# Attention terms on another DMA queue, and first scores behind the reciprocals, in the early batches of a two-layer graph kernel

## The chip, the cores and the metric

The kernel runs on one core of a Trainium2 chip. The metric is the device time of one execution in microseconds, lower is better. TensorE (PE in the profile) multiplies matrices, VectorE (DVE), ScalarE (ACT) and GpSimd (POOL) do element-wise work, SyncE (SP) issues DMA transfers and computes nothing. Each engine works through its own queue of instructions in order. ScalarE and GpSimd can issue DMA transfers too, from the same queue in which their computation stands.

## The reference

x has shape (64, 256, 256): 64 batches of 256 nodes with 256 features; adj is one 256x256 adjacency matrix for all of them. Two layers follow each other, each of a graph attention and a feed-forward part on normalised rows:

```python
x = x + _L0_gnn_ref(_layernorm(x), adj, L0_gnn_W, L0_gnn_a)      # 4 heads of 64
x = x + _L0_ffn_ref(_layernorm(x), L0_ffn_weight, L0_ffn_bias)
x = x + _L1_gnn_ref(_layernorm(x), adj, L1_gnn_W, L1_gnn_a)      # 1 head of 256
x = x + _L1_ffn_ref(_layernorm(x), router_w, w1, b1, w2, b2)     # 2 of 8 experts a row
```

The part that the change touches is the attention of the first layer:

```python
e = e_src[:, :, None, :] + e_dst[:, None, :, :]
e = jnp.where(e >= 0, e, ALPHA * e)
e = jnp.where(mask, e, NEG_INF)
attn = jax.nn.softmax(e, axis=2)
h_prime = jnp.einsum('bijh,bjhd->bihd', attn, q)
```

The last part chooses the two experts of the eight with the highest router scores for each row and adds their outputs, weighted.

## The kernel before

**Tiles.** A batch is two tiles of 128 rows. Each batch is one generator, `batch_layers` (L554), that emits its instructions in about twenty parts. For the most part of the batches, rows are sent by indirect DMA to a region of memory for each expert (L1011), and pairs of 128 rows are fetched, multiplied and added to the output later (`expert_pair`, L829); the last few batches go through all experts densely.

**Order.** The order of instructions is written out by a small scheduler (L1194 to L1235). It works in steps, and a new batch begins every third step. Each active generator has a rank; in one step all of them advance by one part, in order of rank, the lowest first. `yield 10` means: my next part stands in the next step with rank 10. `yield -70` means: my next part stands still in this step, with rank 70. The order in which parts are emitted is the order in which every engine's queue holds them. Nothing of it is decided while the kernel runs.

**The parts of one batch that matter here**, by the step after the batch's begin:

- step 3: `projected` (L573, TensorE, exponentials on ScalarE), then with rank 24 `scaled` (L575, VectorE) and `send_terms` (L577), which turns a small tile ut on VectorE (L505). With rank 31 a DMA writes the 4 KB of ut to DRAM, to `terms` (L579). With rank 52 `spread_terms` (L586, the DMA at L514) reads them back to all 128 partitions, 512 KB into one half of the tile z. So each batch but the first has two DMAs on SyncE's queue for its terms, and the second reads what the first has written.
- step 5: with rank 10, `scores` of heads 0 and 1 (L589), with rank 70 those of heads 2 and 3 (L591). Each is four VectorE instructions at L530 that overwrite z. Batch 0 takes its terms from TensorE and has no such DMA.
- step 7: `attended` of the first layer with rank 50 (L594: TensorE, reciprocals rinv on VectorE at L551), then hp.
- step 8: e on ScalarE (L603), x1 on VectorE.
- steps 9 to 11: norm, transposes, the feed-forward product pf (L618), squares on ScalarE (L402), the copy of a transpose (L427, with rank 36).
- step 12: `projected1` of the second layer with rank 20 (L472; ex, q and me on ScalarE, L479 to L485).
- step 13: `scores1` with rank 25: transposes of ex on TensorE into pd (L491), z1 on VectorE (L496).
- step 14: `attended` of the second layer with rank 40 (L638), with its reciprocals at L551.
- step 15: rel on ScalarE with rank 5 (L644).
- step 18: xng (rank 29) and base (rank 50) on ScalarE (L671, L677).
- steps 19 and 20: the output's base is stored (L688), xng transposed and copied (rank 55), router scores (L702) and their copy lg (L706, rank 35).

Since batches begin three steps apart, step 5 of a batch falls into one step with step 2 of the next (rank 4: a transpose on VectorE), step 8 of the one before (rank 5), step 11 of the second before, step 14 of the third before (rank 40), and step 20 of the fifth before (rank 35). Likewise step 3 falls together with step 15 of the fourth before, step 12 of the third before and step 18 of the fifth before.

**Buffers.** z of the first layer has two buffers, ut one. All products on TensorE go to eight rotating banks of PSUM.

**Chunks and set-up.** `CHUNKS` gives how many batches are routed together: twelve chunks of 4, then smaller ones. Preparation of weights (`setup`, L328) is begun one piece a step from step 4; eight of the pieces are `pack_expert`, with four loads and one store on SyncE's queue each (L281 to L294).

Of the kernel before, what the change touches and what calls it, by code (L numbers as in the profile page):

```python
# [21 lines left out]
def rows_to_all(ap: bass.AP, n: int) -> bass.AP:  # L22

    return bass.AP(tensor=ap.tensor, offset=ap.offset, ap=[[0, P], [1, n]])
# [3 lines left out]
def kernel(  # L28
# [17 lines left out]
    nc = tc.nc  # L46
# [13 lines left out]
    CHUNKS = (4,) * 12 + (2,) * 5 + (1,) * 3  # L60
# [64 lines left out]
        return ap.rearrange("p (a k) -> p k a", k=KT)  # L125

    AHEAD, BLOCKS_AHEAD = 3, 2


    ident = const.tile([P, P], F32, tag="ident", name="ident")  # L130
# [357 lines left out]
    def scores1(ex, me):  # L488
        pd = bank("pd", [N])
        for t in range(NT):  # L490
            nc.tensor.transpose(  # L491
                pd[:, t * P : (t + 1) * P], ex[:, t, 1:2].to_broadcast([P, P]), ident
            )
        z = work.tile([P, NT, N], F32, tag="z1", name="z1", bufs=1)
        for j in range(NT):
            nc.vector.scalar_tensor_tensor(  # L496
                z[:, j, :], pd, ex[:, j, 2:3], me[:, j, :], op0=ALU.max, op1=ALU.mult
            )
        return [z[:, j, :] for j in range(NT)]

    def send_terms(q, b):


        ut = small.tile([P, S], F32, tag="ut", name="ut", bufs=1)
        nc.vector.transpose(  # L505
            ut.rearrange("p (t h w) -> p t h w", t=NT, h=H), q[:, :, :, HD - 1 : HD + 3]
        )
        ud = tc.dram_tile([S, S], F32, name=f"terms_{b}")
        ud = ud.rearrange("c r -> (c r)").rearrange("(c p) -> c p", p=P)
        return ut, ud  # L510

    def spread_terms(ud, z):

        nc.sync.dma_start(  # L514
            out=z[:, NT - 1].rearrange("p t h i -> p (t h i)"),
            in_=rows_to_all(ud, S * S),
        )

    def scores(q, z, hs, spread):

        for h in hs:
            terms = z[:, NT - 1, :, h, :]
            if not spread:
                terms = bank("pd", [NT, P])
                for t in range(NT):
                    nc.tensor.transpose(
                        terms[:, t, :], q[:, t, h, HD + 1 : HD + 2].to_broadcast([P, P]), ident
                    )
            for j in range(NT):
                nc.vector.scalar_tensor_tensor(  # L530
                    z[:, j, :, h, :], terms, q[:, j, h, HD + 2 : HD + 3],
                    masks[0][:, j, :].rearrange("p (t i) -> p t i", t=NT),
                    op0=ALU.max, op1=ALU.mult,
                )
# [19 lines left out]
    def batch_layers(b, c0, xng, lg):  # L554
# [21 lines left out]
        if b:  # L576
            ut, ud = send_terms(q, b)  # L577
            yield -31
            nc.sync.dma_start(  # L579
                out=ud.rearrange("c (g r) -> g c r", g=G),  # L580
                in_=ut[2 : P : S // (NT * H), :],
            )
            yield -52
        z = work.tile([P, NT, NT, H, P], F32, tag="z4", name="z4", bufs=2)
        if b:
            spread_terms(ud, z)  # L586
        yield 99
        yield 10
        scores(q, z, range(0, 2), b > 0)  # L589
        yield -70  # L590
        scores(q, z, range(2, 4), b > 0)  # L591
# [44 lines left out]
        z = scores1(ex, me)  # L636
# [527 lines left out]
    def jobs():  # L1164
        b = done = taken = 0
        for c, nb in enumerate(CHUNKS + (1,) * DENSE):
            nt = nb * NT
            lg = keep.tile([P, nt, E], F32, tag="lg", name=f"lg_{c}", bufs=7)
            xng = []
            row0 = b * N  # L1170
            done += nt
            n = max(done - (E - 1) - taken, 0) if b < ROUTED else 0
            taken += n
            for i in range(nb):
                def job(b=b, c=c, i=i, nb=nb, nt=nt, n=n, lg=lg, xng=xng, row0=row0):
                    yield from batch_layers(b, i * NT, xng, lg)
                    if i == nb - 1:
                        if b >= ROUTED:
                            yield 65
                            yield from route_dense(b, lg)  # L1180
                        else:
                            yield from route(c, row0, nt, n, b == ROUTED - 1, xng, lg)
                yield job()
                b += 1
# [86 lines left out]
```

## Time and profile before

| | |
|---|---|
| three runs | 1525.09, 1535.03, 1537.51 us, median 1535.03 |
| profiled execution | 1543.73 us, span 1542.0 us from the first to the last instruction |
| mean granted TensorE clock | 0.968 of full speed |
| TensorE busy | 1441.8 us, 94% of the span |
| VectorE busy | 1249.1 us, 81% |
| ScalarE busy | 1005.1 us, 65% |
| GpSimd busy | 878.5 us, 57% |
| DMA on the queue of SyncE | 322,828 packets, 171.6 MB |
| writes of terms (L579) and spreads (L514) | 63 each, all on SyncE's queue, median 545 and 350 ns to issue |

The page cuts the span into 40 equal slices; a digit is the busy share of a slice in tenths. Waits name the instruction that waited and the one whose end came last before it went on. In the order of time each row has the start, the length, the engine and line, the operation and its operands, and in brackets the idle time of the engine ahead of it. A small letter q behind an engine's name (SPq, ACTq) marks the engine's queue of DMA issues.

### The profile page before, as it was taken

To read this page: it belongs to the slowest core of one execution; us is meant where nothing else is said; L and a number is where in the kernel's file an instruction comes from. 1 tells how busy PE (TensorE), PEld (TensorE's weight loads), DVE (VectorE), ACT (ScalarE), POOL (GpSimd) and SP (SyncE) were. 2 spreads that over 40 slices of the span, in tenths; PEclk is the share of its full clock that TensorE was granted. 3 is DMA by queue.
4 is the path that set the end of the run, shared out by engine and by line. 5 is a ranking of instruction groups with operands and counts; after the bars stand their busy time and mean duration, and the time that the engine had idled before them with its cause. 6 is when DMAs were issued, how large, how long until landed. Compare 5 with 4: busy or idle time off the path is not lost. (4 is left out here: it accounts for less than half of the span.)

```text
span 1542.0 us, 29896 instructions
## 1 busy us (share of the span) xinstructions
PE 1441.8 (94%) x8066; PEld 1275.5 (83%) x8066; DVE 1249.1 (81%) x4392; ACT 1005.1 (65%) x2379; POOL 878.5 (57%) x853
## 2 busy tenths in 40 slices
PE   7889998999999999999999999998999988789994
PEld 5778787789999898999999989897878777578883
DVE  7779889889988988999889888899887887545542
ACT  1356556477777777777777777776677788544331
POOL 2212344445767766676757575856757677544444
PEclk9989899989999999999999999999999999889998
DMA  5744335557787887787878787867787676788743
GB/s 148 219 126 104 97 107 150 126 145 171 168 182 176 178 170 170 174 184 169 182 165 189 161 194 164 190 143 165 172 183 177 128 156 137 171 171 167 144 78 52
DMA packets 372852, 240.84 MB, mean 156 GB/s; under 512 B 264773, under 2 KB 334925, under 8 KB 372685
## 3 DMA queue, kind: packets, MB, share of 16 engines
q1 hardware_dynamic: 322828, 171.60, 45.2%
q0 software_dynamic: 48864, 66.33, 23.5%
q8 instruction: 67, 1.10, 0.3%
q10 hardware_dynamic: 992, 0.99, 0.2%
q14 instruction: 101, 0.82, 0.2%
HBM read 150.46 MB, written 88.35 MB: 155 GB/s over the span
## 5 line engine op out<-in xcount | busy, mean ns | idle before, releaser
L939 POOL DMA_INDIRECT out_dram<-y,xt x258 | 414.4, 1606 | 192.8 <-issue 63.8
L544 PE MATMUL pv<-q,z 128*128 128x65 f32 (+1 forms) x2560 | 375.0, 303 | 0.2
L544 PEld LDWEIGHTS pv<-q,z 128*128 128x128 f32 x2560 | 343.0, 200 | 12.5 <-DVE z L530 0.6
L1011 POOL DMA_INDIRECT xs<-xng,pos x244 | 266.7, 1093 | 65.3 <-issue 59.8
L918 PE MATMUL py<-w2s,hT 128*128 (+1 forms) x1224 | 285.4, 384 | 6.8 <-ACT hT L909 5.9
L918 PEld LDWEIGHTS py<-w2s,hT 128*128 128x128 f32 x1224 | 231.5, 193 | 39.8 <-ACT hT L909 8.4
L903 PE MATMUL ph<-sT,we 128*128 128x256 f32 x1032 | 240.5, 383 | 6.5 <-DVE sT L117 3.6
L530 DVE SCALAR_TENSOR_TENSOR z<-z,q,mask 128x256 f32<-128x256 f32 x504 | 232.3, 482 | 16.5 <-DMA z<-terms 7.5
L903 PEld LDWEIGHTS ph<-sT,we 128*128 128x128 f32 x1032 | 196.7, 192 | 34.6 <-DVE sT L117 4.4
L427 ACT COPY xT<-pt 128x512 f32<-128x512 f32 x192 | 113.5, 591 | 117.9 <-PE pt L421 93.1
L896 ACT ACTIVATE y<-y,w 128x256 f32<-128x256 f32 x258 | 113.1, 500 | 105.7 <-DVE y L928 98.0
L383 POOL TENSOR_SCALAR rstd<-mv 128x4 f32<-128x4 f32 (+1 forms) x67 | 15.9, 237 | 264.9 <-DVE mv L376 210.0
L909 ACT ACTIVATE hT<-ph,we 128x256 f32<-128x256 f32 x306 | 123.7, 473 | 61.4 <-PE ph L903 41.6
L472 PE MATMUL pq<-wx,xT 128*128 128x259 f32 x512 | 130.5, 398 | 19.0 <-ACT xT L427 15.0
L402 ACT ACTIVATE off<-x,sums 128x256 f32<-128x256 f32 x256 | 129.9, 507 | 16.9 <-DVE x L625 9.6
L928 DVE TENSOR_TENSOR y<-py,b2s 128x512 f32<-128x512 f32 x129 | 85.9, 686 | 58.8 <-PE py L918 45.0
L644 ACT ACTIVATE rel<-pv,rinv 128x256 f32<-128x256 f32 x128 | 53.6, 470 | 121.1 <-DVE rinv L551 95.5
L472 PEld LDWEIGHTS pq<-wx,xT 128*128 128x128 f32 x512 | 96.6, 195 | 41.9 <-ACT xT L427 22.0
L437 PE MATMUL pq<-wx,xT 128*128 128x268 f32 x512 | 128.6, 394 | 2.7 <-DVE xT L117 2.1
L618 PE MATMUL pf<-wfT,xT 128*128 128x256 f32 x512 | 129.4, 398 | 0.0
L437 PEld LDWEIGHTS pq<-wx,xT 128*128 128x128 f32 x512 | 98.6, 193 | 22.3 <-DVE xT L117 1.3
L618 PEld LDWEIGHTS pf<-wfT,xT 128*128 128x128 f32 x512 | 98.5, 203 | 12.3 <-issue 0.2
(164 smaller groups left out, 2373.5 us busy)
## 6 DMA issues: line engine op xcount, KB each, us to landing
we<-wpack SPq DMA_DIRECT2D x145, 288.0 KB
xr<-xs SPq DMA_DIRECT2D x516, 64.0 KB
z<-terms SPq DMA_DIRECT2D x63, 512.0 KB
xblk<-in_x_dram SPq DMA_DIRECT2D x256, 64.0 KB
xin<-in_x_dram SPq DMA_DIRECT2D x64, 256.0 KB
out_dram<-base SPq DMA_DIRECT2D x61, 256.0 KB
out_dram<-y,xt POOLq DMA_INDIRECT x258
xs<-xng,pos POOLq DMA_INDIRECT x244
```

The costliest lines, as they stand in the source:

```text
L402: nc.scalar.activation(off, src[:, t, :], AF.Square, bias=sums[:, t : t + 1], scale=-float(D), accum_out=sq[:, at + t : at + t + 1],)
L427: nc.scalar.copy(dst, pt)
L437: nc.tensor.matmul(pq.rearrange("p h c -> p (h c)"), xT[:, k, t * P : (t + 1) * P], wx[:, k, :], start=(k == 0), stop=(k == KT - 1),)
L472: nc.tensor.matmul(pq, xT[:, k, t * P : (t + 1) * P], wx1[:, k, :], start=(k == 0), stop=(k == KT - 1),)
L530: nc.vector.scalar_tensor_tensor(z[:, j, :, h, :], terms, q[:, j, h, HD + 2 : HD + 3], masks[0][:, j, :].rearrange("p (t i) -> p t i", t=N ...
L544: nc.tensor.matmul(pv[:, h, :], z(j, h, t), q[:, j, h, : d + 1], start=(j == 0), stop=(j == NT - 1),)
L618: nc.tensor.matmul(pf[:, t, :], xT[:, k, t * P : (t + 1) * P], wfT[:, k, :], start=(k == 0), stop=(k == KT - 1),)
L903: nc.tensor.matmul(ph[:, f, :], we[:, k * D + f * P : k * D + (f + 1) * P], xT[:, k, :], start=(k == 0), stop=(k == KT - 1),)
L909: nc.scalar.activation(hT[:, f, :], ph[:, f, :], AF.Gelu, bias=we[:, C_B1 + f : C_B1 + f + 1])
L918: nc.tensor.matmul(py[:, t, :], hT[:, f, t * P : (t + 1) * P], w2s[:, e, f * D : (f + 1) * D].rearrange("p e c -> p (e c)"), start=(f == 0 ...
L939: d = nc.gpsimd.indirect_dma_start(out=out_rows, out_offset=bass.IndirectOffsetOnAxis(ap=xt[:, t, 0:1].bitcast(I32), axis=0), in_=y[:, t, ...
L1011: d = nc.gpsimd.indirect_dma_start(out=xs_d[: E * CAP * PAIR, :], out_offset=bass.IndirectOffsetOnAxis(ap=at, axis=0), in_=xe, in_offset=None,
```

## The change

Two limits are computed from the chunks: `PAIRED` is 4 + 4 + 3 = 11, `SETTLED` is 16 + 2 = 18.

Both DMAs of a batch's terms, the write of ut and the spread into z, go to the queue of ScalarE (`nc.scalar`) in batches 1 to 17 and stay on that of SyncE from batch 18 on. Their ranks, 31 and 52, stay.

In batches 0 to 10 the scores of heads 0 and 1 get rank 42 in place of 10. In their step they then stand behind the second layer's reciprocals (rank 40) of the batch three before, and behind lg (rank 35) of the one five before. The scores of heads 2 and 3 keep rank 70.

```diff
     AHEAD, BLOCKS_AHEAD = 3, 2
+    PAIRED = CHUNKS[0] + CHUNKS[1] + 3
+    SETTLED = CHUNKS[0] + CHUNKS[1] + CHUNKS[2] + CHUNKS[3] + 2
...
-    def spread_terms(ud, z):
-
-        nc.sync.dma_start(
+    def terms_queue(b):
+
+        return nc.scalar if b < SETTLED else nc.sync
+
+    def spread_terms(b, ud, z):
+
+        terms_queue(b).dma_start(
             out=z[:, NT - 1].rearrange("p t h i -> p (t h i)"),
             in_=rows_to_all(ud, S * S),
         )
...
             yield -31
-            nc.sync.dma_start(
+            terms_queue(b).dma_start(
                 out=ud.rearrange("c (g r) -> g c r", g=G),
                 in_=ut[2 : P : S // (NT * H), :],
             )
             yield -52
         z = work.tile([P, NT, NT, H, P], F32, tag="z4", name="z4", bufs=2)
         if b:
-            spread_terms(ud, z)
+            spread_terms(b, ud, z)
         yield 99
-        yield 10
+        yield 10 if b >= PAIRED else 42
         scores(q, z, range(0, 2), b > 0)
         yield -70
         scores(q, z, range(2, 4), b > 0)
```

## The prediction

> **What bounds the kernel now.** I read the page's slices first, then clock and engines by stretch, and last the waits and the order of time of the first 450 us: the terms of batches 1 to 17 are issued from 22.8 to 280.1 us, so everything the change moves happens there.
>
> ```profile
> PE   7889998999999999999999999998999988789994
> ...
> PEclk9989899989999999999999999999999999889998
> ```
>
> A slice is 38.5 us. TensorE is full from slice 9 on, the first eight have gaps, and the granted clock dips there. The chain that ended last lies in the drain and says nothing of this start. Columns of the next view: the stretch, its length, busy us of PE, weight loads, VectorE, ScalarE, GpSimd, the granted clock, DMA share, GB/s.
>
> ```profile
> 77.70:81.10 3.40, 0.00 (x0) 0.00 (x0) 2.25 (x7) 0.29 (x1) 0.00 (x0) 1.00 0.78 272
> 81.10:91.30 10.20, 9.40 (x41) 8.92 (x42) 6.96 (x27) 5.98 (x17) 1.38 (x3) 0.50 0.75 209
> 91.30:169.90 78.60, 76.35 (x476) 67.20 (x476) 72.92 (x249) 50.25 (x141) 17.90 (x29) 1.00 0.37 90
> ```
>
> From 91 to 170 us VectorE works 72.9 of 78.6 us, and the order of time shows it without a gap over 0.31 us after 93 us: it is the bound there, TensorE follows. Reordering takes nothing from its work, so **only VectorE's own idle time can be won** before 200 us. It stands in two kinds of place: waits for terms, and waits for a TensorE at half clock. The order of time around the worst, SyncE's queue alone and then the engines:
>
> ```profile
> 69.90 0.53 SPq L579 DMA_DIRECT2D terms<-ut  x1
> 70.47 0.44 SPq L96 DMA_DIRECT2D xin<-in_x_dram  x1
> 74.06 0.34 SPq L514 DMA_DIRECT2D z<-terms  x1
> ```
>
> ```profile
> 78.77 1.92 DVE L530 SCALAR_TENSOR_TENSOR z<-z,q,mask 128x256 f32<-128x256 f32 x4 [5.70 <-DMA z<-terms]
> ...
> 80.81 0.84 ACT L644 ACTIVATE rel<-pv,rinv 128x256 f32<-128x256 f32 x2 [8.42 <-DVE rinv L551]
> ...
> 81.86 0.99 PE L491 MATMUL pd<-ident,ex 128*128 128x128 f32 x2 [5.16 <-ACT ex L479]
> ...
> 89.61 0.18 DVE L551 RECIPROCAL rinv<-pv 128x4 f32<-128x4 f32 x1 [2.81 <-PE pv L544]
> ...
> 92.78 0.48 DVE L625 SCALAR_TENSOR_TENSOR x<-pf,rstd,x1b 128x256 f32<-128x256 f32 x1 [1.67 <-PE pf L618]
> ```
>
> Batch 4's terms lie ready in ut at 66.1, but SyncE is busy with block loads and the packs of experts and sends them at 69.9; the spread waits for the write until 74.06. The bytes are back at 78.8. VectorE stands 5.70 us at the first scores; the second layer's reciprocals of batch 1 are behind them, so ScalarE's rel (8.42) and TensorE's transposes of ex (5.16) stand too. Then TensorE runs 10.2 us at clock 0.50, and VectorE waits for it twice more, 2.81 + 1.67 = 4.48 us. The sums of the first 450 us (total, times, longest):
>
> ```profile
> ACT rel L644 <- DVE rinv L551: 75.2, 21, 8.4
> ...
> ACT e L603 <- DVE hp L597: 25.2, 14, 7.6
> ...
> DVE z L530 <- DMA z<-terms: 7.5, 3, 5.7
> ```
>
> **What the Trainium skill says.** "DMA: Bandwidth & Descriptors", section Issuing engines are not separate DMA queues: transfers from any queue run on the same 16 engines and interleave; another issuing engine saves issue time alone. So I don't count on more bandwidth, only on leaving SyncE's line; no run here shows the interleaving yet. Same page, section Anatomy of one DMA: a semaphore wait is held by the issuing sequencer, not by the DMA engine. The trace agrees: in the same 450 us SyncE itself waits for terms at L514, 22.0 us in 24 times. "TensorE: Matmul & The Clock Gate", section Part 1: after an idle window of about 3.4 us the clock falls to half. The trace agrees: 77.7 to 81.1 is wholly idle, 81.1 to 91.3 has 0.50.
>
> **The change part by part.**
>
> 1. *Terms of batches 1 to 17 off SyncE's queue.* 34 DMAs move: 17 writes (median 545 ns of issue) and 17 spreads (350 ns). Waits for them: 1.63 us at 60.06 (batch 3), 5.70 (batch 4), 0.19 at 110.01 (batch 6), 7.5 in all. Batch 3: ut is ready at 50.4, SyncE wrote at 52.09, spread at 55.60. From ScalarE: written 50.4, spread by 53.9 at the latest (the 3.5 us SyncE needed), landed 4.5 later (55.60 to 60.06) at 58.4, which is when VectorE gets there. Gain 1.6. Batch 4: written 66.1, spread 1.7 (the usual step, 129.65 to 131.33) to 4.2 us later (69.90 to 74.06), landed 4.5 to 5.8 later (104.23 to 110.01): 72.3 to 76.1, against 73.1 when VectorE gets there. Gain 2.7 to 5.7; I take 4.5, as the DMA engines stay loaded with the packs. Sum **-6.1 us** (bounds 4 to 7.5).
>
> 2. *First scores behind the reciprocals, batches 1 to 10* (batch 0 too, which finds no second layer yet). Nothing is added: four instructions of L530, 1.91 us a group, change places with lg (0.17) and two reciprocals (0.22). The second pair of scores stays, so z is complete when it was. The new risk is a VectorE that waits for pv: ahead of the scores of batches 8 to 10, pv of the batch three before is done at 136.4, 150.9 and 166.4, and VectorE arrives at 136.85, 152.8, 168.8; no wait. rel and ex come up to 1.9 us earlier. TensorE's waits for ex then go (1.43 at 63, 5.16 at 82, 0.64 at 156, 1.67 at 172), but where VectorE is the bound this is worth nothing by itself. Its worth is the clock: without the idle 77 to 82, which part 1 alone would mostly remove as well, the half clock that follows goes and with it 4.48 us of VectorE's waits: **-4.5** (bounds 0 to 4.5). The stretch from 173.3 to 183.5, again at 0.50, follows a weaker gap, 1.47 + 0.20 of idle beside transposes, and costs VectorE 1.48 at 179.11 and 2.84 at 183.45, together 4.3. Windows fall by chance, so I take two thirds: **-2.9** (0 to 4.3; with the stretch at 193.7, another 0.44 + 2.42 = 2.9, it may be 7.2).
>
> 3. *What ScalarE pays.* 17 x (0.545 + 0.350) = 15.2 us of issue. ScalarE's five shapes of DMA at the start took 0.34 to 0.53, so bounds are 0.2 to 1.0 each. It also waits: for ut hardly, since its own xT copy ends as ut does (129.99 and 129.6 in batch 8); for the write to land 1.7 us, of which base (1.14, L677) covers most; take 0.5, in a loaded queue 2. That is 17 x 1.4 = 24 us on ScalarE. Queued behind it: the copy of xng's transpose (TensorE's router product waits), y of an expert, e (VectorE's L607), the squares (GpSimd's rstd), the copy before L472. The cover is idle time at just these: 25.2 us in 14 times before e, about 1.8 each, and the 3.6 a batch before rel. In batch 8's period e has only 0.26 of idle, the shift of 0.3 to 0.5 reaches the copy at 135.29, and TensorE is in pv until 136.44 while that copy ended at 135.85: hidden by 0.1 to 0.3 us. Batches 11 to 17 keep the old order and 1.7 us before e. Price on the path **+1** (bounds 0 to 10).
>
> 4. *What SyncE gains.* It no longer stands for ut with xin, base stores, xblk, packs and expert loads behind. No engine waits for those in this stretch beyond 1.0 us at the very start: **0**; POOL's queue is not passed.
>
> Sum: -6.1 - 4.5 - 2.9 + 1 = -12.5 us. From 320 us on TensorE is full and the program's order is fixed, so the shift should arrive at the end. The profiled execution took 1543.73 us (span 1542.0 and 1.7 around it), giving 1531.2; it is 8.7 above the median of 1535.03, and the median becomes **1522.5, say 1523**.
>
> **Rivals.** *The clock follows wholly*: the stretches at 81, 173 and 194 all vanish: -7.5 - 4.5 - 7.2 = -19, 1516. For it: each follows a wait for ex; against: batch 11, right before 194, keeps the old order. *The stall stays*: the packs saturate the DMA engines, the bytes land as late, and VectorE stands as before; only batch 3 and part of the clock are won: -3, 1532. *Slower: ScalarE held at the head of its queue.* Each of 17 batches has 0.9 of issue and 0.8 of wait (22.0/24 is 0.9 on SyncE) on ScalarE just ahead of e and the copies. If all is exposed, 17 x 1.7 = 29 less the 7.5 won is +21: 1556. It decides once the delay exceeds ScalarE's idle before e, 1.8 us on average but 0.26 in batch 8, and once TensorE's larger waits bring back half-clock stretches. Against: VectorE, not ScalarE, is the bound there. That the moves don't take effect at all I hold for very unlikely, as the order is written out.
>
> **Chances.** A measurement of this kernel can tell about 1%, 15 us, from no change. Forecast 0.52 (own range 1517 to 1530), clock follows 0.25, stall stays 0.12, slower 0.11. Faster by over 1% (under 1519.7): 0.25 and 0.12 of the forecast's, 0.37. Within 1%: 0.40 + 0.12 = 0.52. Slower: 0.11. The range from 1510 (the second case and 6 us, the spread of the runs shown) to 1538 (the third and 6) leaves out 2 in 10.
>
> **What would show it.** In the changed profile: L579 and L514 of early batches on ScalarE's queue, the write within 0.5 us of ut; no wait of z for terms over 2 us; rel's wait for rinv from about 3.6 down to under 2 us up to batch 10, and as before in 11 to 17; no idle of TensorE over 3 us near 80 and no clock of 0.5 right behind. Wrong if z still waits over 4 us, if the clock dips as often, or if ScalarE's copies make L472, e or hT late.

## The result, and the profile after

| | before | after |
|---|---|---|
| median, 20 runs each on one chip | 1533.6 us (1525.09 to 1546.77) | 1524.84 us (1517.67 to 1536.17) |
| ratio, with its 95% interval | | 0.9952 [0.9934, 0.9969] |
| profiled execution, and its span | 1543.73 us, 1542.0 us | 1526.76 us, 1525.0 us |
| mean granted TensorE clock in it | 0.968 | 0.976 |

The change makes the kernel 0.48% faster: less than the 1% bound of the prediction, yet an interval that leaves 1 out. Most lines stand six lower in the new file: z L536 (was L530), the write of ut L585 (L579), the spread L520 (L514), e L609 (L603), reciprocals L557 (L551), rel L650 (L644), while the copy xT is L429 (L427), the second layer's product L474 (L472), transposes of ex L493 (L491).

First the page of the changed kernel: busy tenths of TensorE and its clock in 40 slices of 38.1 us, then two queues with packets, megabytes and share of the DMA engines' time.

```profile
PE   6899989899999999999999999998999888779996
...
PEclk9999998999999999999999999999999999889998
...
q1 hardware_dynamic: 319768, 162.62, 43.6%
...
q10 hardware_dynamic: 4052, 9.98, 2.0%
```

The dips of the clock in slices 3, 5 and 9 are gone, one in slice 7 (229 to 267 us) is new. Queue q10, with 992 packets and 0.99 MB before, now carries 3,060 packets and 9 MB more, and q1 as much less: the 34 transfers of terms have moved.

Next the waits of the first 450 us (total us, times, longest).

```profile
ACT rel L650 <- DVE rinv L557: 51.3, 21, 5.2
...
ACT e L609 <- DVE x L612: 10.4, 1, 10.4
...
ACT xT L429 <- DMA terms<-ut: 5.4, 6, 1.9
...
ACT e L609 <- DVE x L656: 5.1, 1, 5.1
...
DVE z L536 <- DMA z<-terms: 4.0, 2, 2.2
```

The wait that the change aims at, z for terms, shrank from 7.5 to 4.0 us but is not gone. rel's wait fell from 75.2 to 51.3. Three lines are new: ScalarE now waits for its own write of ut (`DMA terms<-ut`) by name, and twice its e starts late "for x", which e does not read in the program. The order of time around the first of these, batch 2, shows what really held it.

```profile
35.11 0.21 DVE L507 STREAM_TRANSPOSE ut<-q 128x32 f32<-128x32 f32 x1
...
35.35 0.52 ACTq L585 DMA_DIRECT2D terms<-ut  x1
35.38 0.36 SPq L296 DMA_DIRECT2D wpack<-wt  x1
...
35.78 0.43 SPq L283 DMA_DIRECT2D wt<-in_L_ffn_w_dram  x1
...
39.90 0.38 SPq L287 DMA_DIRECT2D wt<-in_L_ffn_b_dram  x1
39.91 0.38 ACTq L520 DMA_DIRECT2D z<-terms  x1
...
40.40 0.63 ACT L609 ACTIVATE e<-hp 128x512 f32<-128x512 f32 x1 [10.37 <-DVE x L612]
...
42.67 3.82 PE L474 MATMUL pq<-wx,xT 128*128 128x259 f32 x8 [3.44 <-ACT xT L429]
...
44.71 3.75 DVE L536 SCALAR_TENSOR_TENSOR z<-z,q,mask 128x256 f32<-128x256 f32 x8 [2.23 <-DMA z<-terms]
```

The write leaves 0.03 us after ut is turned, as it should. But the spread behind it on the same queue goes out 4.56 us later, once the write has landed, and until then nothing else of ScalarE's queue can start: e, the squares and the copy xT stand. So TensorE's product for the second layer waits 3.44 us for the copy (0.89 in the kernel before), and z of this batch waits 2.23 us for its terms, where the profile of before shows no such wait. SyncE's queue in that profile, at the same batch:

```profile
36.50 0.53 SPq L579 DMA_DIRECT2D terms<-ut  x1
...
38.22 0.34 SPq L514 DMA_DIRECT2D z<-terms  x1
38.66 0.37 SPq L294 DMA_DIRECT2D wpack<-wt  x1
39.08 0.42 SPq L281 DMA_DIRECT2D wt<-in_L_ffn_w_dram  x1
```

There the write took 1.72 us, and the pack's store and the next load went out behind the spread. Once the terms have left SyncE's line, store and load go out 0.03 and 0.43 us after the write, beside it. All profiles agree: batch 2's step from write to spread is 4.05 to 4.79 us in the seven with its terms on ScalarE's queue, 1.71 to 1.76 in the seven with them on SyncE's, three of which load the packs as densely as here. That it is the pack's bytes that slow the write is a reading of this order, not a test of its own. Nor is SyncE rid of the terms: its next load waits until 39.90, when the write has landed. Why it does isn't shown.

In batch 3 write and spread are 2.00 us apart (50.61 and 52.61), behind which e waits for hp anyway. In batches 4 and 5 (same view) it is again more:

```profile
65.09 0.53 ACTq L585 DMA_DIRECT2D terms<-ut  x1
67.96 0.35 ACTq L520 DMA_DIRECT2D z<-terms  x1
...
73.92 3.75 DVE L536 SCALAR_TENSOR_TENSOR z<-z,q,mask 128x256 f32<-128x256 f32 x8 [1.75 <-DMA z<-terms]
...
79.93 0.52 ACTq L585 DMA_DIRECT2D terms<-ut  x1
...
83.10 0.33 ACTq L520 DMA_DIRECT2D z<-terms  x1
...
83.47 0.59 ACT L429 COPY xT<-pt 128x512 f32<-128x512 f32 x1 [1.88 <-DMA terms<-ut]
...
84.11 1.06 PE L708 MATMUL pl<-rT,xT 128*128 128x8 f32 x8 [1.93 <-ACT xT L429]
```

Write to spread takes 2.87 us in batch 4 and 3.17 in batch 5. Batch 4's z waits 1.75 us where it waited 5.70. In batch 5 the router's product on TensorE is 1.93 us late, through the copy queued behind the spread. Last the clock by stretch, in the columns of the prediction:

```profile
41.80:48.60 6.80, 5.93 (x14) 4.62 (x15) 4.42 (x11) 3.14 (x10) 0.98 (x2) 0.50 0.80 257
86.20:89.60 3.40, 3.40 (x10) 2.65 (x9) 1.75 (x6) 2.07 (x7) 1.20 (x2) 0.50 0.85 326
91.30:169.90 78.60, 75.62 (x490) 67.55 (x489) 74.11 (x262) 52.82 (x142) 18.86 (x30) 1.00 0.34 103
```

The first stretch begins 2.6 us into TensorE's gap of 3.44, the second 2.1 us after the one of 1.93. Up to 100 us that makes 10.2 us of half clock. Before had 20.4: the 10.2 at 81.1, and 6.8 at 33.3 and 3.4 at 43.5 besides. From 91 to 170 us VectorE works 74.1 of 78.6 us; it is still the bound there.

**Where the time came from.** A plain measure: the start of ut's transposition in each batch, minus the same start in the profile of before.

| batch | 1 | 3 | 4 | 5 | 6 | 11 | 12 | 16 | 19 to 40 | end of span |
|---|---|---|---|---|---|---|---|---|---|---|
| us | -1.2 | +0.2 | -1.0 | -5.0 | -7.8 | -7.7 | -12.2 | -8.3 | about -11.5 | -17.0 |

Some 6.6 us are won between batches 1 and 6, none of it before batch 4. Nothing changes from 6 to 11. Then comes the clock: before had half clock at 173.3 and 193.7 us, after at 181.8 and 229.6, and so the gain rises and falls back. Two further profiles of the changed kernel gave -6.6 and -4.9 us between batches 1 and 6. A single pair of profiles says little about the end: the three of the changed kernel took 1521.18, 1526.76 and 1534.23 us, and the pair compared here is 17.0 us apart, the medians 8.8.

### The profile page after: what moved, and what is told of

Read it like the earlier page. It is cut to its first block, busy times and chain, and to the rows that moved or that the text cites. A ratio compares the mean times of both kernels' runs of the same rounds, so it can differ in the third digit from the quotient of the medians.

```text
span 1525.0 us, 29925 instructions
## 1 busy us (share of the span) xinstructions
PE 1430.2 (94%) x8066; PEld 1265.0 (83%) x8066; DVE 1248.0 (82%) x4392; ACT 1006.8 (66%) x2379; POOL 876.8 (57%) x853
## 5 line engine op out<-in xcount | busy, mean ns | idle before, releaser
L550 PE MATMUL pv<-q,z 128*128 128x65 f32 (+1 forms) x2560 | 369.7, 300 | 0.4
L550 PEld LDWEIGHTS pv<-q,z 128*128 128x128 f32 x2560 | 336.5, 196 | 13.1 <-DVE z L536 1.1
L536 DVE SCALAR_TENSOR_TENSOR z<-z,q,mask 128x256 f32<-128x256 f32 x504 | 231.5, 482 | 13.1 <-DMA z<-terms 4.0
L429 ACT COPY xT<-pt 128x512 f32<-128x512 f32 x192 | 113.1, 589 | 113.4 <-PE pt L423 73.2
L474 PE MATMUL pq<-wx,xT 128*128 128x259 f32 x512 | 130.1, 397 | 21.5 <-ACT xT L429 19.0
L474 PEld LDWEIGHTS pq<-wx,xT 128*128 128x128 f32 x512 | 96.6, 195 | 45.1 <-ACT xT L429 26.6
L624 PE MATMUL pf<-wfT,xT 128*128 128x256 f32 x512 | 125.5, 389 | 0.0
L650 ACT ACTIVATE rel<-pv,rinv 128x256 f32<-128x256 f32 x128 | 53.7, 469 | 97.5 <-DVE rinv L557 68.6
```

The costliest lines, as they stand in the source:

```text
L429: nc.scalar.copy(dst, pt)
L474: nc.tensor.matmul(pq, xT[:, k, t * P : (t + 1) * P], wx1[:, k, :], start=(k == 0), stop=(k == KT - 1),)
L536: nc.vector.scalar_tensor_tensor(z[:, j, :, h, :], terms, q[:, j, h, HD + 2 : HD + 3], masks[0][:, j, :].rearrange("p (t i) -> p t i", t=N ...
L550: nc.tensor.matmul(pv[:, h, :], z(j, h, t), q[:, j, h, : d + 1], start=(j == 0), stop=(j == NT - 1),)
L624: nc.tensor.matmul(pf[:, t, :], xT[:, k, t * P : (t + 1) * P], wfT[:, k, :], start=(k == 0), stop=(k == KT - 1),)
```

## The experiments

Three groups of four kernels each shared a median of before: 1531.62 us (51 runs), 1533.58 (28) and 1528.36 (44). Since that median moves, ratios and kernels of one group are compared. Edits are to the changed kernel unless said otherwise; an interval is that of the ratio to before.

### Each part alone

The queue alone, with the old order of scores:

```diff
-    PAIRED = CHUNKS[0] + CHUNKS[1] + 3
+    PAIRED = 0
```

> Terms of batches 1 to 17 on ScalarE's queue, the scores at rank 10 everywhere. Theory 1 (the stall for terms is what was won, and it is SyncE's line that made it): z's wait for terms of 5.7 us at batch 4 falls to under 2.5, TensorE's idle of 5.2 us near 80 us and the half clock behind it go, VectorE is some 5 to 7 us ahead of the kernel before by batch 6, and the time is 5 to 8 us lower. Theory 2 (the order alone does it, the queue only changes the carrier): under 2 us by batch 6 and no change in time.

Measured: 1526.29 us, ratio 0.998 [0.996, 1.0]. By batch 6 its profile is 7.5 us ahead of before, and z waits for terms 4.4 us in all, 2.3 at the longest.

The order alone, with all terms on SyncE's queue:

```diff
-    SETTLED = CHUNKS[0] + CHUNKS[1] + CHUNKS[2] + CHUNKS[3] + 2
+    SETTLED = 0
```

> Scores of batches 0 to 10 behind the reciprocals, all terms on SyncE's queue. Theory 1: z still waits for terms about 5.5 us at batch 4, so VectorE is no further ahead by its own wait; but rel no longer stands behind that wait, TensorE does not idle over 3 us near 80 us, and the half clock behind it with VectorE's 4.5 us of waits goes: 3 to 5 us ahead by batch 6, 3 to 5 us off the time. Theory 2: 7 to 8 us ahead, as with both. Rival (VectorE is the bound, the order is worth nothing): within 1 us of before.

Measured: 1529.75 us, ratio 0.9989 [0.9974, 1.0004]; batch 6 is 2.3 us further ahead than batch 1 is. The order of time on VectorE in this kernel:

```profile
76.84 3.76 DVE L536 SCALAR_TENSOR_TENSOR z<-z,q,mask 128x256 f32<-128x256 f32 x8 [3.65 <-DMA z<-terms]
...
89.14 0.48 DVE L631 SCALAR_TENSOR_TENSOR x<-pf,rstd,x1b 128x256 f32<-128x256 f32 x1 [2.84 <-PE pf L624]
```

Batch 4's scores still wait 3.65 us for terms. What no longer waits is the work that used to stand behind them: the reciprocals are emitted ahead. But half clock came all the same, from 79.2 us for 10.2 us, and VectorE pays it with 2.84 us of waiting for TensorE, nearly the 2.81 of before. So the order doesn't remove that stretch. The order alone is no change that can be told, and the queue alone, whose interval just reaches 1, hardly one; run again (below), it gave nearly the same.

### More and fewer batches on ScalarE's queue

Every batch:

```diff
-    SETTLED = CHUNKS[0] + CHUNKS[1] + CHUNKS[2] + CHUNKS[3] + 2
+    SETTLED = B
```

> As the changed kernel, but all 63 batches' terms on ScalarE's queue. Prices what ScalarE pays per batch where TensorE is the bound (batches 18 to 58). If the cover holds there too: equal to the changed kernel within 3 us. If ScalarE's wait for the write to land (1.7 us and more in a loaded DMA) reaches hT, y or the copies: 46 more batches at 0.3 to 1 us, 14 to 46 us slower than the changed kernel, and TensorE's waits for hT or xT grow.

Measured: 1548.55 us, ratio 1.0126 [1.009, 1.0163], against 0.9952 for the changed kernel: 1.7% of 1531.6 is 27 us lost over 46 more batches, about 0.58 us each (the two intervals allow 0.45 to 0.71). Waits of TensorE between 350 and 1330 us, first in this kernel, then in the kernel before:

```profile
PE pq L474 <- ACT xT L429: 21.3, 10, 5.2
PE pq L474 <- issue: 10.9, 6, 2.6
```

```profile
PE pq L472 <- ACT xT L427: 12.5, 10, 3.0
...
PE pq L472 <- issue: 2.8, 3, 1.9
```

The second layer's product waits for the copy xT, or with no releaser that the profile names ("issue"): 32.2 us where it was 15.3. Eight waits of this product, of 2.1 to 2.6 us and 18.2 in all, come once in four batches between 389 and 973 us, where the kernel before has none over 0.4. The chain behind one of them, and then a wait of SyncE's queue in this kernel from 350 to 1330 us:

```profile
459.79 0.32 SPq L851 DMA_DIRECT2D xr<-xs  x1
459.80 0.35 ACTq L520 DMA_DIRECT2D z<-terms  x1
...
464.64 0.71 DVE L117 STREAM_TRANSPOSE sT<-xr 128x512 f32<-128x512 f32 x1 [2.74 <-DMA xr<-xs]
...
467.02 0.63 ACT L609 ACTIVATE e<-hp 128x512 f32<-128x512 f32 x1 [3.30 <-DVE hp L603]
...
473.46 2.02 PE L474 MATMUL pq<-wx,xT 128*128 128x259 f32 x8 [2.16 <-ACT xT L429]
```

```profile
SPq L851 <- DMA terms<-ut: 65.6, 9, 9.1
```

The last load of an expert's rows, on SyncE's queue, goes out with the spread, once the write has landed on ScalarE's. So the rows come late, VectorE waits for them, hp behind them is late, e waits for hp (31.9 us in this stretch, 9.8 in the kernel before), and the copy xT stands behind e in ScalarE's queue. In all eight the loads of rows go out within 0.03 us of the spread and e waits 3.2 to 3.8 us for hp. ScalarE itself is hardly held by the terms here: one write left at 645.28 us, its spread at 646.94, just as base between them (from 645.84, 1.09 us) ended. Why a load on SyncE's queue waits for a write on ScalarE's the runs don't show. **The price of the move in a stretch where TensorE is full is about 0.58 us a batch, and most of what the trace places of it comes by SyncE's loads, not by a ScalarE held at its queue.** The kernel loses steadily: 20.6 us ahead of before in its own profile at batch 23, 6.2 behind at the end.

Only the two batches whose waits the profile of before shows:

```diff
-        return nc.scalar if b < SETTLED else nc.sync
+        return nc.scalar if b in (3, 4) else nc.sync
```

> As the changed kernel, but only batches 3 and 4 have their terms on ScalarE's queue, the two whose terms came late. Theory 1 (only those two are worth anything, the other fifteen cost ScalarE a little): at least as far ahead by batch 6 as the changed kernel, 7 to 10 us, as the wait for batch 2's terms (2.2 us after the change) does not come up, and the time 0 to 4 us below the changed kernel. Rival (the other fifteen free SyncE's queue for other loads and are worth something): 2 us or more above the changed kernel.

Measured: 1531.61 us, ratio 0.9994 [0.9975, 1.0012]. Nothing is won: batch 5 starts 5.2 us earlier than before, and by batch 6 only 1.2 of it are left, by batch 7 it is a us behind. SyncE's queue, then VectorE, in this kernel:

```profile
85.64 0.65 SPq L317 DMA_DIRECT2D out_dram<-fill  x1
86.34 2.14 SPq L106 DMA_DIRECT2D xblk<-in_x_dram  x4
88.57 0.56 SPq L585 DMA_DIRECT2D terms<-ut  x1
...
90.32 0.34 SPq L520 DMA_DIRECT2D z<-terms  x1
```

```profile
79.47 0.21 DVE L507 STREAM_TRANSPOSE ut<-q 128x32 f32<-128x32 f32 x1
...
95.34 1.92 DVE L536 SCALAR_TENSOR_TENSOR z<-z,q,mask 128x256 f32<-128x256 f32 x4 [8.51 <-DMA z<-terms]
```

Batch 5's ut was ready at 79.7 us. SyncE, still at the last packs of experts (ended by the fills of `xs` and `out_dram`), sent it at 88.57, and z waited 8.51 us. Of the 8.9 us between, SyncE stood 3.9 at the last pack's store, which waits for its own loads. The stall had moved one batch on. That the cost sits at batches 3 and 4, as I read the profile of before, fell with this run: **those waits are the front of a backlog on SyncE that lasts until the packs are out, near 88 us.**

Batches 1 to 5, the ones inside the backlog:

```diff
-    SETTLED = CHUNKS[0] + CHUNKS[1] + CHUNKS[2] + CHUNKS[3] + 2
+    SETTLED = 6
```

> The changed kernel with only batches 1 to 5 on ScalarE's queue. If twelve more batches (6 to 17) neither pay nor win, as VectorE is the bound there: equal to the changed kernel within 2 us. If ScalarE pays there 0.58 us a batch as in batches 18 to 63 (26.8 us over 46): 7 us below the changed kernel.

Measured: 1526.57 us, ratio 0.9958 [0.994, 0.9976]; the changed kernel of the same group gave 1524.78 and 0.994 [0.9918, 0.9962]. A price of 0.58 us in each of batches 6 to 17 would have put it 7 us below. The intervals overlap widely: nothing can be told of these batches, and 7 us are not there.

### The backlog taken away at its source

Pieces of the set-up, the packs among them, are begun in every third step from step 8 on, not in every one. The rest is the kernel before, with neither part of the change:

```diff
-            if step >= SETUP_AT and setup:
+            if step >= SETUP_AT and setup and (step < 8 or step % TICKS == 1):
```

> The kernel before, with the eight packs of experts begun one in every third step (steps 10 to 31) in place of one in every step (8 to 15); terms on SyncE's queue, scores at rank 10. Theory 1, amended (the stall is SyncE's backlog of packs in steps 8 to 16; taking terms of all batches in that time off its queue and thinning the packs are two cures of one thing): z's waits for terms after 45 us under 1 us in all, no idle of TensorE over 3 us near 80 us, VectorE 7 to 9 us ahead by batch 6, and the time 4 to 8 us below before, as with the queue alone or better, since ScalarE pays nothing. Rival (the load of the DMA engines by other transfers is the cause, not the line): z still waits 3 us or more in batches 3 to 6, the time within 2 us of before.

Measured: 1521.29 us, ratio 0.9919 [0.9895, 0.9942], a gain of 12 us. SyncE's queue in this kernel, at batch 4:

```profile
63.48 0.51 SPq L579 DMA_DIRECT2D terms<-ut  x1
...
65.20 0.34 SPq L514 DMA_DIRECT2D z<-terms  x1
```

Write to spread is 1.72 us, against 4.16 in the kernel before, and no z waits for terms at all. Batch 6 comes 11.5 us further ahead than batch 1 does, about twice the gain of the change. From 45 to 120 us, this kernel and then the one before:

```profile
45.00:120.00 75.00, 73.60 (x465) 64.93 (x465) 69.82 (x232) 46.20 (x129) 16.06 (x26) 0.99 0.56 156
```

```profile
45.00:120.00 75.00, 66.81 (x388) 58.49 (x386) 58.61 (x194) 38.07 (x107) 13.34 (x21) 0.92 0.58 160
```

The DMA engines are as busy on the mean (0.56 and 0.58, 156 and 160 GB/s), yet VectorE does 69.8 us of work in place of 58.6. The mean isn't what the terms met, though: while batch 4's write was under way the DMA engines were busy 0.04 of the time here, 0.74 in the kernel before. So thinning took away two things, 3.8 us of standing in line and 2.4 us of landing, and these runs don't tell what each was worth. "DMA: Bandwidth & Descriptors", section Issuing engines are not separate DMA queues, says that transfers of all queues share the same 16 engines and that more issuing engines save issue time alone, "usually small". The first half fits batch 2 of the changed kernel: its write on ScalarE's queue took 4.56 us while SyncE's loads were moving and the DMA engines were busy 0.86 of the time. For the second, what counted here was not an instruction's 0.5 us of issue but the 3.8 us of the line of loads ahead of it.

The same thinned packs with the change's order of scores, all terms on SyncE:

```diff
-    SETTLED = CHUNKS[0] + CHUNKS[1] + CHUNKS[2] + CHUNKS[3] + 2
+    SETTLED = 0
...
-            if step >= SETUP_AT and setup:
+            if step >= SETUP_AT and setup and (step < 8 or step % TICKS == 1):
```

> As the one before, with the scores of batches 0 to 10 behind the reciprocals. If the order's worth is fewer half-clock stretches up to batch 10: 2 to 5 us below the kernel with thinned packs alone, and 0 to 4 us below the changed kernel. If the order is worth nothing once the stall is gone: within 1.5 us of the kernel with thinned packs alone.

Measured: 1522.13 us, ratio 0.9934 [0.9904, 0.9964]. The order up to batch 10 adds nothing that can be told to the thinned packs.

### Does the order pay on top of the queue?

The changed kernel, the queue alone and the thinned packs alone were run again in one group. The changed kernel's second run had stood in the group of the thinned packs' first.

> The changed kernel once more, as the measure for the others on this chip: ratio 0.993 to 0.997 to the kernel before.

> The changed kernel, beside the queue alone on one chip: 0.994 to 0.996 of the kernel before.

> The queue alone a second time, on the chip of the changed kernel. If the order adds to the queue (4 us between the two so far, on different chips, intervals that touch): 3 us or more above the changed kernel again. If that was chance: within 2 us of it.

> The thinned packs alone a second time, as the version to beat: 0.990 to 0.994 of the kernel before, 3 to 6 us below the changed kernel.

| | us | ratio to before |
|---|---|---|
| changed kernel, second | 1524.78 | 0.994 [0.9918, 0.9962] |
| changed kernel, third | 1520.16 | 0.9945 [0.9926, 0.9965] |
| queue alone, again | 1524.01 | 0.9978 [0.9956, 1.0] |
| thinned packs, again | 1517.57 | 0.9934 [0.99, 0.9967] |

The order on top of the queue was worth 0.9978 to 0.9945 in one group, and 0.998 to 0.9952 across two: some 4 to 5 us both times, with intervals that overlap. The traces don't show where. From batch 1 to 6 they even speak against the order: the queue alone gains 7.5 and 7.6 us, the changed kernel 6.6, 6.6 and 4.9. In all three profiles of the changed kernel the router's product near 84 us waits 1.93 to 2.20 us for the copy xT and a stretch of half clock follows, of 3.4 to 6.8 us; in both of the queue alone it waits 0.85 and 0.88, and none follows before 293 us. Half clock, worked out as 2 x (1 - mean clock) x time over all runs, is 69 to 70 us in both queue-only runs and 69 to 75 in three of the changed kernel. Where those 4 us come from stays open.

### Both cures, and the order further

Thinned packs, terms on SyncE, and the scores behind the reciprocals up to batch 19:

```diff
-    PAIRED = CHUNKS[0] + CHUNKS[1] + 3
-    SETTLED = CHUNKS[0] + CHUNKS[1] + CHUNKS[2] + CHUNKS[3] + 2
+    PAIRED = 20
+    SETTLED = 0
...
-            if step >= SETUP_AT and setup:
+            if step >= SETUP_AT and setup and (step < 8 or step % TICKS == 1):
```

> Thinned packs, and the scores of batches 0 to 19 behind the reciprocals; all terms on SyncE's queue. TensorE's waits for ex (0.4 to 2.1 us a batch from 170 to 310 us) should go, and with them half-clock stretches between 170 and 320 us: if these are what the order is worth, 3 to 6 us below the thinned packs alone. If the order is worth nothing, or VectorE then waits for pv where TensorE has experts' products ahead of it: equal or up to 5 us above.

Measured: 1515.07 us, ratio 0.9917 [0.9888, 0.9946], the lowest time of its group. It is faster than the kernel before, and its six runs (1508.85 to 1517.38) all lie below the changed kernel's 1520.16 beside it, though the intervals overlap. Against the thinned packs alone (0.9934) it isn't told apart by its interval. What the order does is plain, though. Waits of TensorE from 100 to 330 us, thinned packs alone and then with the order:

```profile
PE pd L491 <- ACT ex L479: 8.7, 16, 1.9
PE pt L421 <- DVE x L625: 4.3, 6, 0.9
```

```profile
PE pt L423 <- DVE x L631: 11.1, 8, 2.1
PE pq L474 <- ACT xT L429: 3.9, 2, 2.0
```

The 16 waits for ex vanish, and waits for VectorE's x take their place: 11.1 us for 4.3. In all TensorE waits 15.0 us there in place of 16.2. That is what a reorder does here: it chooses who waits.

## Why the prediction was right, and where it was not

The time came out 1.8 us above the forecast of 1523, inside the range; the gain was 0.48% where 0.8% was forecast. Steps 1 and 2 promised 10.6 us by batch 6; three profiles show 6.6, 6.6 and 4.9. That the sum comes as near as it does is in part luck: by the medians some 4 of the 8.8 us won came with the order on top of the queue, at no place that the prediction names.

- **Terms off SyncE's queue, -6.1.** The mechanism held: writes leave within 0.1 us of ut, and batch 4's wait fell from 5.70 to 1.75 us, a gain of 3.95 where 4.5 was taken. Batch 3's 1.63 went, but 2.23 came at batch 2, so z's waits fell by 3.5 us in all. The sign "no wait of z for terms over 2 us" was missed by this one.
- **The half clock after 81.1 us, -4.5.** Of 10.2 us 3.4 came back, at 86.2, behind TensorE's wait of 1.93. From batch 4 to 6, which holds batch 4's wait and this stretch, the changed profile gains 6.8 us; 4.5 + 4.5 = 9.0 was promised. Less the 3.95 of the wait, 2.8 are left for the clock.
- **The mis-sized term** is in step 3: "for the write to land 1.7 us, of which base (1.14, L677) covers most; take 0.5, in a loaded queue 2". From write to spread it took 4.56, 2.00, 2.87 and 3.17 us in batches 2 to 5, most of it with ScalarE standing, and reached TensorE as waits of 3.44 and 1.93 us. The "+1" on the path stood for this. It was taken for all 17 batches alike, when the hold is long in the packs' stretch and no cost shows after it.
- **The rival "ScalarE held at the head of its queue"** has a mechanism that the runs show, but in batches 2 to 5 alone, not in 6 to 17, where moving the terms back to SyncE changed nothing that can be told. From 18 on the run with all batches does lose 0.58 us a batch, mostly by another path: SyncE's loads of rows wait for the write. The claim that batches 11 to 17 are covered held.
- **The order.** That it is worth nothing where VectorE is the bound holds for the order alone (0.9989 [0.9974, 1.0004]) and for the order on thinned packs. On top of the queue some 4 us showed up that I can't place. rel's wait up to batch 10 fell to between 0.29 and 1.53 us up to 129 us, then to 2.35 and 2.88: lower than 3.1 to 8.4, not always under 2.
- **The stretch at 173.3, -2.9.** It went in this profile, and stretches of 6.8 us at 181.8 and 10.2 at 229.6 came. Half clock over all runs, in the two groups that hold both kernels, fell from 79.9 to 75 us and from 76.4 to 69; these 5 to 7 us, at the 0.33 to 0.44 us below, are some 2 to 3 us. Both clock terms together were put at 7.4. Which stretch goes could not be read from one profile.
- **SyncE gains nothing, 0.** The reason given for step 4 doesn't hold: it says that SyncE "no longer stands for ut with xin, base stores, xblk, packs and expert loads behind". In the first 100 us of the changed profile it still waits 16.1 us in six times for the write of the terms and 14.4 in four for the spread. Nor is the effect nothing: in batch 2 the pack's loads went out sooner and beside the write. And the step asked too little. SyncE's loads made the stall; thinning them won 10.8 to 12.3 us with no other change, 2.6 and 3.5 us more than the change beside it, though with intervals that overlap. The prediction saw SyncE "busy with block loads and the packs" and did not ask whether they had to stand there.

## What to carry to other kernels

When a transfer is late, look first at what stands ahead of it in its own queue, and whether that must go out just then; spacing out the loads there won at least as much as moving the late transfer to a compute engine's queue. A write followed by a read of the same bytes holds a compute engine for the landing time of the write, and here that was longest in just the stretch where the move seemed to pay. Ask too what goes out sooner once the transfer has left the line, and whether the line is really free of it. Before a wait is removed by hand in the batches that show it, ask what is behind it: with a backlog, the next batch waits.

## What the runs showed of the hardware

- The step from the 4 KB write to the spread that waits for it was 1.72 us with thinned packs (batch 4, DMA share 0.04 meanwhile), and 4.56, 2.00, 2.87 and 3.17 in batches 2 to 5 of the changed kernel (shares 0.86, 0.72, 0.82 and 0.89), though ScalarE's queue carried hardly anything but terms. Another queue doesn't shield a transfer from the others' bytes. The share alone doesn't settle the time: batch 2 of the kernel before took 1.72 us at 0.77.
- With all terms on ScalarE's queue, SyncE's queue stood and its next issue began within 0.03 us of the spread in 38 of 63 batches. So in this kernel a queue that no longer carried a transfer still stood for it; the cause is open.
- Half clock came in lengths of 3.4, 6.8, 10.2 and 13.7 us only, but for the last stretch of each profile, which ends with the span. It also followed gaps of TensorE shorter than that: in the 3.4 us ahead of the falls at 41.9, 86.2 and 229.6 TensorE was busy 0.77, 2.13 and 1.78 us, and ahead of the one at 33.3 in the kernel before 3.20. "TensorE: Matmul & The Clock Gate", Part 1, speaks of a whole idle window of about 3.4 us; the fall at 81.1 in the kernel before agrees with that, these four do not.
- Over 51 runs of the kernel before, one more microsecond of half clock (from the mean clock) went with about 0.33 us more time, correlation 0.79; in the two other groups of before with 0.33 and 0.44 (0.72 and 0.82). So the clock goes with more than half of the spread between runs, and a third of its length or somewhat more goes with it in time, rather than half.
